# First attention of a four-layer network: weighing one unit later, output rows transposed in the bank of the sums, and preparation work as single steps inside the loop

## The chip, the core and the metric

The kernel runs on one core of a Trainium2 chip. The metric is the device time of one execution in microseconds (us). A core has five engines with a queue of instructions each: TensorE (PE; the profile lists its weight loads apart, as PEld), VectorE (DVE), ScalarE (ACT), GpSimd (POOL) and SyncE (SP), which here only starts transfers. Every queue runs in order; an instruction that needs another engine's result waits on a semaphore, and all that stands behind it in its queue waits with it. Matmuls read SBUF and write PSUM, which is divided into banks of 512 float32 values per partition.

## The reference: what is computed

Four layers follow one another. Each computes a mixing part s and a gate part from the layer-normed input xn, and adds `x + s * silu(ffn(xn))`. The change lies in the first layer and in work that prepares weights for the later ones. The first layer's s is a sliding-window attention over 8 sequences of 512 tokens with 128 features, 16 heads of 8 features and blocks of 64 queries, each of which sees its own block of keys and the block before:

```
q, k, v = proj(Wq, bq), proj(Wk, bk), proj(Wv, bv)      # 16 heads of 8
scores = einsum("bhnqd,bhnkd->bhnqk", qb, kw) * hd ** -0.5   # 64 queries x 128 keys
valid = (t <= s_ + W) & (t >= s_ + 1) & (n * W - W + t >= 0)
attn = softmax(where(valid, scores, -1e9))
out = einsum("bhnqk,bhnkd->bhnqd", attn, vw) ; return out @ Wo.T + bo
```

The first layer's gate part uses six 128x128 weights that come as integers and are decoded: `(q / 7.5 - 1) * scale`. The second layer mixes each token with the one before it (`hidden * time_mix + shifted * (1 - time_mix)`), which the kernel folds into scaled weight copies. The fourth layer's attention uses 16 sigmoid and softplus values per head (mu, sigma, eta, gamma, nu).

## The kernel before

`network` loads x in 8 parts, the constants of all layers, and the attention weights; then it runs `layer_norm`, the preparations `l0_decode`, `l2.fill` and `l1.fill`, `l0_attention`, `l0_ffn`, and from there the later layers. The data lie with features on partitions and tokens along the free axis.

Two kinds of order meet. Instructions that go through `net.in_order(engine)` stay on their queue in the order in which the program makes them. All others (plain `nc.vector`, `nc.scalar`) are placed by a scheduler, among the ordered ones. The layer norm and the attention are ordered. The decoding (`l0_decode`, L2828 to L2830, tile wt from f_q and sc), and the scalars of the fourth layer (`l3_scalars`, from L2875, tiles sp and mu) are free, so the scheduler puts them early: into the layer norm and in front of the attention. The mixing weights of the second layer (`L1Consts.fill`, tiles td, rest and wm, and the halved fourth weight) are ordered on ACT, before the attention, and the two large expert weights (m1_w13 and m1_w2, 2560 and 1280 KB, tile m_w) are started from ACT's queue.

The attention works in 64 units: sequence (batch) b, pair m of query blocks, and half hh of the heads; eight units are one batch. Unit u goes through these steps:

- `scores(u)`: four matmuls into one sc tile of two banks (two such tiles); DVE scales and masks (e<-sc), finds the row maximum (mx), POOL subtracts it. Runs three units ahead.
- Exp on ACT, two units ahead.
- `turned(u)`: eight transposes into two tp tiles, each copied by ACT to pt.
- `weigh(u)`: 32 small matmuls of pt with the values vw, into the tile av: the sums of 16 heads and, in a ninth column, their total. Its two halves alternate between pairs.
- After the second unit of a pair: `norm` (DVE rec and o), `out_rows` (one transpose tpo, and ACT's copy with a bias to ot), and after the last pair of a batch `finish` (ps_o and DVE s).
- `project(b + 1)` makes the next batch's keys, queries and values a step per unit: ps_k with four masked key copies kb (DVE, ACT, DVE, ACT), ps_q with ACT q, and two ps_v with ACT vw.

PSUM's eight banks are used up: four for sc, three in rotation for tp, tpo, ps_k, ps_q, ps_v and ps_o, one for the sums.

The loop gives the order in all queues; an iteration is turned(u), norm, scores(u + 3), out_rows, Exp(u + 2), weigh(u), finish, and one step of project:

```
for u in range(N + 2):
    ended = u >= 1 and u <= N and u % 2 == 0
    if u < N: pts = turned(u)
    if ended: o = norm(u - 1)
    if u + AHEAD < N: scores(u + AHEAD)
    if ended: out_rows(u - 1, o)
    if u + 2 < N: act.activation(e[u + 2], e[u + 2], AF.Exp)
    if u < N: weigh(u, pts)
    if u >= U and u % U == 1: finish(u // U - 1)
    next(todo, None)
```

Of the kernel before, what the change touches and what calls it, by code (L numbers as in the profile page):

```python
# [257 lines left out]
def l0_attention(net, xn, s_out, p0, w, bias):  # L258
# [6 lines left out]
    with ExitStack() as st:  # L265
# [23 lines left out]
        sums = p_av.tile([P, 2, H, HD + 1], F32, tag="av", name="av")  # L289
# [6 lines left out]
        def project(b):  # L296
# [6 lines left out]
            for c in range(4):  # L303
                hm, hb = net.hm4[:, c : c + 1], kbias[:, c : c + 1]
                if c % 2:
                    act.activation(kb[b][:, c, :], ps, AF.Identity, scale=hm, bias=hb)
                    yield
                else:
                    dve.tensor_scalar(kb[b][:, c, :], ps, hm, hb, ALU.mult, ALU.add)
            ps = p_t.tile([P, S], F32, tag="t", name="ps_q")  # L310
# [47 lines left out]
        def turned(u):  # L358

            pts = []  # L360
            for g in range(2):
# [3 lines left out]
                pt = p3.tile([P, 4, P], F32, tag="pt", name="pt")  # L365
# [28 lines left out]
        def out_rows(u, o):  # L394
            b, m = u // U, u // 2 % 4
            tp = p_t.tile([P, 4, P], F32, tag="t", name="tpo")
            pe.transpose(tp[:, 0, :], o.rearrange("p h d -> p (h d)"), net.ident)
            if m == 0:
                ot[b] = p2.tile([P, S], F32, tag="ot", name="ot")

            act.activation(ot[b][:, ts(m, P)], tp[:, 0, :], AF.Identity, bias=bias[:, 2:3])
# [12 lines left out]
        act.activation(e[1], e[1], AF.Exp)  # L414
        todo = iter(())
        for u in range(N + 2):
            if u < N and u % U == 0 and u // U + 1 < B:
                todo = project(u // U + 1)
            ended = u >= 1 and u <= N and u % 2 == 0
            if u < N:  # L420
                pts = turned(u)
            if ended:
                o = norm(u - 1)
            if u + AHEAD < N:
                scores(u + AHEAD)
            if ended:
                out_rows(u - 1, o)
            if u + 2 < N:
                act.activation(e[u + 2], e[u + 2], AF.Exp)
            if u < N:  # L430
                weigh(u, pts)
            if u >= U and u % U == 1:
                finish(u // U - 1)
            next(todo, None)
            if u == 4 * U:
# [3 lines left out]
            if u > 4 * U and u % U == 6:  # L439
                next(low, None)  # L440

# [290 lines left out]
class L1Consts:  # L732
    E = 8

    def __init__(self, net, st):
        nc, tc, E = net.nc, net.tc, self.E
        self.net = net
        self.p1 = p1 = st.enter_context(tc.tile_pool(name="a1_c", bufs=1))
# [7 lines left out]
    def fill(self):  # L746
        net, nc, p1, E = self.net, self.net.nc, self.p1, self.E
        act = net.in_order(nc.scalar)
        self.w13 = net.load(p1, "m1_w13", act)
        self.w2 = net.load(p1, "m1_w2", act)  # L750

        w, par = self.w, self.par
        self.td = td = p1.tile([P, 1], F32, tag="td", name="td")
        act.activation(td, par[:, 0:1], AF.Exp)
        act.activation(td, td, AF.Copy, scale=-1.0)
        self.tf = par[:, 1:2]
        self.wm = wm = p1.tile([P, 3, 2, P], F32, tag="wm", name="wm")
        self.rest = rest = p1.tile([P, 3], F32, tag="rest", name="rest")
        act.activation(rest, par[:, 2:5], AF.Identity, scale=-1.0, bias=net.ones[:, 0:1])
        for i in range(3):  # L760
            act.activation(wm[:, i, 0, :], w[:, i, :], AF.Copy, scale=par[:, 2 + i : 3 + i])
            act.activation(wm[:, i, 1, :], w[:, i, :], AF.Copy, scale=rest[:, i : i + 1])
        act.activation(w[:, 3, :], w[:, 3, :], AF.Copy, scale=0.5)
# [22 lines left out]
        nc.gpsimd.memset(self.keep[:, :, 0:1], 0.0)  # L786

# [554 lines left out]
class L2Consts:  # L1342
# [4 lines left out]
    def __init__(self, net, st):  # L1347
# [5 lines left out]
        self.p1 = p1 = st.enter_context(tc.tile_pool(name="a2_c", bufs=1))  # L1353
# [1442 lines left out]
class Prepared:  # L2796
# [29 lines left out]
    def l0_decode(self):  # L2826
        nc, wt, qw, sc = self.net.nc, self.f0_wt, self.qw, self.sc
        nc.vector.tensor_copy(wt, qw)  # L2828
        nc.vector.tensor_scalar(wt, wt, 1.0 / 7.5, -1.0, ALU.mult, ALU.add)
        nc.vector.tensor_tensor(wt, wt, sc, ALU.mult)  # L2830
# [34 lines left out]
    def l3_scalars(self):  # L2865
# [9 lines left out]
        nc.vector.scalar_tensor_tensor(sp, raw, -1.0, raw, ALU.mult, ALU.min)  # L2875
        nc.scalar.activation(sp, sp, AF.Exp)
        nc.scalar.activation(sp, sp, AF.Ln, bias=net.ones[:, 0:1])
        nc.vector.scalar_tensor_tensor(sp, raw, 0.0, sp, ALU.max, ALU.add)
        sig2, eta2, gam2, nu = (sp[:, i, :] for i in range(4))

# [4 lines left out]
        nc.scalar.activation(mu, par[:, 0, :], AF.Exp, scale=-1.0)  # L2885
        nc.vector.tensor_scalar(mu, mu, 1.0, None, ALU.add)
        nc.vector.reciprocal(mu, mu)
        nc.vector.tensor_scalar(mu, mu, 1e-4, None, ALU.add)
        nc.vector.tensor_scalar(nmu, mu, -1.0, None, ALU.mult)

        nc.vector.tensor_scalar(v_e2, nmu, 2.0, None, ALU.mult)
        nc.vector.reciprocal(v_e2, v_e2)
        nc.vector.tensor_tensor(v_e2, v_e2, sig2, ALU.mult)
        nc.vector.tensor_tensor(v_0, eta2, gam2, ALU.add)
        nc.vector.tensor_tensor(v_0, v_0, v_e2, ALU.subtract)
        nc.vector.tensor_scalar(coef, nu, float(DH), -0.5, ALU.add, ALU.mult)
        nc.vector.tensor_tensor(coef, coef, par[:, 5, :], ALU.mult)


        norm_0 = vec("norm_0")  # L2900
# [124 lines left out]
```

## Time and profile before

| | |
|---|---|
| median of 9 runs | 2329.14 us (2323.07 to 2332.13) |
| profiled execution: time, span | 2332.06 us, 2330.3 us |
| busy in the span | PE 2180.1 (94%), DVE 2003.8, ACT 1846.5, POOL 1571.0 us |
| layer norm ends, first ps_k | 29.91 us |
| first scores of the attention | 42.6 us |
| ps_k of the next batches | 55.95, 97.95, 129.79, 161.7 us, then about 193.6, 226, 259 |
| first feed-forward matmul | 321.26 us |
| PE busy from 42.6 to 319.4 | 259.59 of 276.80 us, mean granted clock 0.92 |

The profile shows each instruction with its start, length, tiles (output <- inputs), shape and, in square brackets, how long its engine stood before it and whom it waited for. A granted clock of 1.00 is the full speed of TensorE, 0.50 half of it. In the windows, the columns are the busy times and counts of PE, PEld, DVE, ACT and POOL, then the granted clock, the share of the transfer engines and GB/s. The chain of waits lists start, length and what the time went to, in the chain that ended last. The page's first lines and its slices for the span:

```profile
span 2330.3 us, 48928 instructions
...
PE 2180.1 (94%) x17762; PEld 1523.3 (65%) x17762; DVE 2003.8 (86%) x3595; ACT 1846.5 (79%) x3882; POOL 1571.0 (67%) x1410
...
PE   5999998999987999869999999999999999999998
...
PEclk7899989899998999989999999999999999999998
```

A slice is 58 us, so the first holds the layer norm and the lead-in, and the next five the attention.

### The profile page before, as it was taken

How to read it: one execution, taken by the hardware profiler on the slowest of the kernel's cores; microseconds unless marked ns; L12 is line 12 of the kernel's file. 1: busy time of each engine (PE TensorE's matmuls, PEld its weight loads, DVE VectorE, ACT ScalarE, POOL GpSimd, SP SyncE). 2: the span in 40 equal slices, each digit the busy share in tenths (PEclk: the TensorE clock that was granted, in tenths of full speed). 3: DMA queues.
4: the chain of work that ended last, by engine and by line, in shares of the span. 5: the costliest groups of instructions: out<-in, count | busy, mean ns of one | idle time of the engine just before them, and what ended most of it. 6: DMA issues, size and time to landing. Idle time of an engine off the chain costs nothing.

```text
span 2330.3 us, 48928 instructions
## 1 busy us (share of the span) xinstructions
PE 2180.1 (94%) x17762; PEld 1523.3 (65%) x17762; DVE 2003.8 (86%) x3595; ACT 1846.5 (79%) x3882; POOL 1571.0 (67%) x1410
## 2 busy tenths in 40 slices
PE   5999998999987999869999999999999999999998
PEld 4666675656634666636777777777777777777796
DVE  4577769785687999659999999999999999999885
ACT  4566655555544899838999999999999999999974
POOL 5344436264276788656788788888788888788644
PEclk7899989899998999989999999999999999999998
DMA  4000000012210000234433444434444444443100
GB/s 144 2 2 2 2 1 23 17 54 70 46 50 16 3 17 16 81 84 108 106 100 92 111 114 105 106 92 107 109 108 105 100 105 107 102 102 101 46 1 37
DMA packets 91618, 156.94 MB, mean 67 GB/s; under 512 B 20145, under 2 KB 44465, under 8 KB 91121
## 3 DMA queue, kind: packets, MB, share of 16 engines
q1 hardware_dynamic: 86736, 140.95, 23.2%
q0 software_dynamic: 4352, 8.92, 1.5%
q10 hardware_dynamic: 288, 3.93, 0.4%
q8 instruction: 142, 2.33, 0.4%
q14 instruction: 100, 0.81, 0.1%
HBM read 30.52 MB, written 12.06 MB: 18 GB/s over the span
## 4 chain that ended last, share of the span: by engine, by line
PE 55%; DVE 28%; POOL 7%; issue 4%; ACT 4%; DMA 2%; SPq 1%; DVEq 0%; ACTq 0%; POOLq 0%
PE sc L84 10%; DVE sc L84 7%; DVE r L84 6%; DVE y L84 6%; PE ps_av L84 5%; PE tp L84 5%; PE ps_kq L84 4%; PE ps_u L84 4%; PE av L84 3%; PE ps_ab L84 3%; PE ps_n L84 2%; DVE mx L84 2%; DVE e L84 2%; PE ps_v L84 2%; POOL yr L84 2%
## 5 line engine op out<-in xcount | busy, mean ns | idle before, releaser
L84 POOL TENSOR_TENSOR ek<-E,kn 128x512 f32<-128x512 f32 (+3 forms) x512 | 433.6, 869 | 204.1 <-DMA kn<-nr 186.0
L84 POOL TENSOR_TENSOR e<-e,mx 128x1024 f32<-128x1024 f32 x112 | 212.1, 1899 | 188.4 <-DVE mx L84 95.5
L84 PE MATMUL sc<-r 128*128 128x512 f32 (+3 forms) x1024 | 312.5, 449 | 25.9 <-DVE y L84 23.0
L84 POOL TENSOR_TENSOR r<-r,rs 128x1024 f32<-128x1024 f32 x128 | 303.7, 2374 | 23.8 <-DMA rs<-r 20.9
L84 PE MATMUL ps_av<-u,at 128*128 128x128 f32 x2560 | 306.8, 275 | 0.3 <-DVE at L84 0.3
L84 PEld LDWEIGHTS ps_av<-u,at 128*128 128x128 f32 x2560 | 296.1, 192 | 1.5 <-ACT at L84 0.8
L84 PEld LDWEIGHTS sc<-r 128*128 128x128 f32 x1024 | 166.7, 193 | 191.4 <-issue 123.6
L84 ACT ACTIVATE y<-y,mn 128x384 f32<-128x384 f32 (+3 forms) x512 | 288.5, 569 | 4.0 <-DVE mn L84 3.2
L84 DVE CUSTOM_DVE_ANT_0 y<-y,ps_g,ncs 128x256 f32<-128x256 f32 (+3 forms) x512 | 253.8, 541 | 0.8 <-ACT y L84 0.8
L84 DVE SCALAR_TENSOR_TENSOR y<-sc,qn,V 128x512 f32<-128x512 f32 (+3 forms) x512 | 246.8, 544 | 8.6
L84 ACT ACT_TABLE_LOAD x179 | 229.7, 1283 | 6.1 <-DVE ex L84 2.1
L84 PEld LDWEIGHTS tp<-ident,y 128*128 128x128 f32 x1280 | 161.0, 141 | 112.3 <-issue 48.5
L84 PE MATMUL tp<-ident,y 128*128 128x128 f32 x1280 | 202.5, 274 | 2.6 <-ACT o L84 2.0
L84 DVE SCALAR_TENSOR_TENSOR sc<-sc,ek 128x1280 f32<-128x1280 f32 x128 | 189.7, 1482 | 9.7 <-PE sc L84 3.1
L84 ACT COPY at<-tp 128x512 f32<-128x512 f32 x376 | 191.3, 509 | 7.6 <-PE tp L84 3.5
L84 DVE TENSOR_TENSOR sc<-sc,EF 128x1280 f32<-128x1280 f32 x128 | 191.9, 1499 | 4.3
L84 ACT ACTIVATE y<-y 128x1280 f32<-128x1280 f32 x128 | 163.4, 1277 | 6.0 <-DVE y L84 2.9
L84 DVE TENSOR_TENSOR r<-sn,ps_kq 128x1024 f32<-128x1024 f32 x128 | 155.1, 1212 | 9.9 <-ACT sq L84 9.9
L84 ACT ACTIVATE sq<-ps_kq 128x1024 f32<-128x1024 f32 x128 | 131.5, 1027 | 35.4 <-PE ps_kq L84 35.4
L84 DVE TENSOR_TENSOR r<-ct,ps_kq 128x1024 f32<-128x1024 f32 x128 | 155.1, 1212 | 0.0
L84 POOL TENSOR_TENSOR s<-s,o 128x512 f32<-128x512 f32 x116 | 148.2, 1277 | 2.5 <-ACT o L84 2.4
L84 ACT ACTIVATE e<-e 128x1024 f32<-128x1024 f32 x112 | 117.3, 1061 | 40.4 <-POOL e L84 40.0
(462 smaller groups left out, 5012.5 us busy)
## 6 DMA issues: line engine op xcount, KB each, us to landing
rs<-r SPq DMA_DIRECT2D x256, 256.0 KB, 3.8
kn<-nr SPq DMA_DIRECT2D x512, 64.0 KB, 2.0
yrows<-yy SPq DMA_DIRECT2D x36, 128.0 KB, 1.8
ct<-trig SPq DMA_DIRECT2D x16, 256.0 KB
EF<-E SPq DMA_DIRECT2D x16, 256.0 KB, 2.5
EF<-E SPq DMA_DIRECT2D x16, 192.0 KB
m_w<-m_w ACTq DMA_DIRECT2D x1, 2560.0 KB, 10.2
x<-x SPq DMA_DIRECT2D x8, 256.0 KB, 4.7
```

Source lines behind the costliest of these rows:

```text
L84: ins = op(*args, **kwargs)
```

## The change

- The loop weighs unit u - 1 in iteration u. The pt tiles come from a ring of four in place of three; the steps that follow the weighing (norm, out_rows, finish) move back by one iteration, and the loop is one longer.
- tpo has no bank of its own. It becomes 128 columns behind the sums, in their tile (`both`, named av).
- The key copies are made in the order ACT, DVE, ACT, DVE, with a pause of project after each DVE copy.
- Decoding, the mixing weights and the scalars become generators whose instructions are ordered on their queues; the loop takes one of their 17 steps in three iterations of every batch from u = 9. The last operation of the decoding goes from DVE to POOL. The low-rank steps come one iteration earlier.
- The constants of the second and third layer are loaded after those of the first, and the two large expert weights are started from SP's queue.

```diff
--- before.py
+++ after.py
@@ -255,7 +255,7 @@
             )
 
 
-def l0_attention(net, xn, s_out, p0, w, bias):
+def l0_attention(net, xn, s_out, p0, w, bias, l1):
 
 
     nc, tc = net.nc, net.tc
@@ -286,7 +286,10 @@
             nc.gpsimd.memset(vw, 1.0)
             vws.append(vw)
 
-        sums = p_av.tile([P, 2, H, HD + 1], F32, tag="av", name="av")
+        both = p_av.tile([P, TB], F32, tag="av", name="av")
+        n_av = 2 * H * (HD + 1)
+        sums = both[:, 0:n_av].rearrange("p (m h d) -> p m h d", m=2, h=H)
+        tpo = both[:, n_av : n_av + P]
 
         pe, dve, act, pool = (
             net.in_order(e) for e in (nc.tensor, nc.vector, nc.scalar, nc.gpsimd)
@@ -300,13 +303,13 @@
             pe.matmul(ps, lhsT=w[:, 1, :], rhs=xb, start=True, stop=True)
 
             kb[b] = p2.tile([P, 4, S], F32, tag="kb", name="kb")
-            for c in range(4):
+            for c in (1, 0, 3, 2):
                 hm, hb = net.hm4[:, c : c + 1], kbias[:, c : c + 1]
                 if c % 2:
                     act.activation(kb[b][:, c, :], ps, AF.Identity, scale=hm, bias=hb)
-                    yield
                 else:
                     dve.tensor_scalar(kb[b][:, c, :], ps, hm, hb, ALU.mult, ALU.add)
+                    yield
             ps = p_t.tile([P, S], F32, tag="t", name="ps_q")
             pe.matmul(ps, lhsT=w[:, 0, :], rhs=xb, start=True, stop=True)
             q[b] = p2.tile([P, S], F32, tag="q", name="q")
@@ -362,7 +365,7 @@
                 tp = p_t.tile([P, 4, P], F32, tag="t", name="tp")
                 for j in range(4):
                     pe.transpose(tp[:, j, :], e[u][:, 4 * g + j, :], net.ident)
-                pt = p3.tile([P, 4, P], F32, tag="pt", name="pt")
+                pt = p5.tile([P, 4, P], F32, tag="pt", name="pt")
                 act.copy(pt, tp)
                 pts.append(pt)
             return pts
@@ -393,12 +396,11 @@
 
         def out_rows(u, o):
             b, m = u // U, u // 2 % 4
-            tp = p_t.tile([P, 4, P], F32, tag="t", name="tpo")
-            pe.transpose(tp[:, 0, :], o.rearrange("p h d -> p (h d)"), net.ident)
+            pe.transpose(tpo, o.rearrange("p h d -> p (h d)"), net.ident)
             if m == 0:
                 ot[b] = p2.tile([P, S], F32, tag="ot", name="ot")
 
-            act.activation(ot[b][:, ts(m, P)], tp[:, 0, :], AF.Identity, bias=bias[:, 2:3])
+            act.activation(ot[b][:, ts(m, P)], tpo, AF.Identity, bias=bias[:, 2:3])
 
         def finish(b):
             ps = p_t.tile([P, S], F32, tag="t", name="ps_o")
@@ -412,32 +414,43 @@
             scores(u)
         act.activation(e[0], e[0], AF.Exp)
         act.activation(e[1], e[1], AF.Exp)
+        def early():
+            yield from net.prep.l0_decode(dve, pool)
+            yield from l1.mixing(act)
+            yield from net.prep.l3_scalars(dve, act)
+
+        rest = early()
         todo = iter(())
-        for u in range(N + 2):
+        pts = {}
+        for u in range(N + 3):
             if u < N and u % U == 0 and u // U + 1 < B:
                 todo = project(u // U + 1)
-            ended = u >= 1 and u <= N and u % 2 == 0
+            ended = u >= 3 and u % 2 == 1
             if u < N:
-                pts = turned(u)
+                pts[u] = turned(u)
             if ended:
-                o = norm(u - 1)
+                o = norm(u - 2)
             if u + AHEAD < N:
                 scores(u + AHEAD)
             if ended:
-                out_rows(u - 1, o)
+                out_rows(u - 2, o)
             if u + 2 < N:
                 act.activation(e[u + 2], e[u + 2], AF.Exp)
-            if u < N:
-                weigh(u, pts)
-            if u >= U and u % U == 1:
+            if 1 <= u <= N:
+                weigh(u - 1, pts.pop(u - 1))
+            if u >= U and u % U == 2:
                 finish(u // U - 1)
             next(todo, None)
+            if u >= U and u % U in (1, 3, 6):
+                next(rest, None)
             if u == 4 * U:
                 low = net.prep.l0_low_rank(
                     p0, lambda name: p_t.tile([P, S], F32, tag="t", name=name), pe, dve, act
                 )
-            if u > 4 * U and u % U == 6:
+            if u > 4 * U and u % U == 5:
                 next(low, None)
+        for _ in rest:
+            pass
 
 
 L0_FFN = (
@@ -735,7 +748,10 @@
     def __init__(self, net, st):
         nc, tc, E = net.nc, net.tc, self.E
         self.net = net
-        self.p1 = p1 = st.enter_context(tc.tile_pool(name="a1_c", bufs=1))
+        self.p1 = st.enter_context(tc.tile_pool(name="a1_c", bufs=1))
+
+    def load(self):
+        net, nc, p1, E = self.net, self.net.nc, self.p1, self.E
         self.rw = net.load(p1, "m1_r")
         self.eb = p1.tile([P, E], F32, tag="eb", name="eb")
         nc.sync.dma_start(self.eb, net.ins["m1_eb"].partition_broadcast(P))
@@ -745,22 +761,8 @@
 
     def fill(self):
         net, nc, p1, E = self.net, self.net.nc, self.p1, self.E
-        act = net.in_order(nc.scalar)
-        self.w13 = net.load(p1, "m1_w13", act)
-        self.w2 = net.load(p1, "m1_w2", act)
-
-        w, par = self.w, self.par
-        self.td = td = p1.tile([P, 1], F32, tag="td", name="td")
-        act.activation(td, par[:, 0:1], AF.Exp)
-        act.activation(td, td, AF.Copy, scale=-1.0)
-        self.tf = par[:, 1:2]
-        self.wm = wm = p1.tile([P, 3, 2, P], F32, tag="wm", name="wm")
-        self.rest = rest = p1.tile([P, 3], F32, tag="rest", name="rest")
-        act.activation(rest, par[:, 2:5], AF.Identity, scale=-1.0, bias=net.ones[:, 0:1])
-        for i in range(3):
-            act.activation(wm[:, i, 0, :], w[:, i, :], AF.Copy, scale=par[:, 2 + i : 3 + i])
-            act.activation(wm[:, i, 1, :], w[:, i, :], AF.Copy, scale=rest[:, i : i + 1])
-        act.activation(w[:, 3, :], w[:, 3, :], AF.Copy, scale=0.5)
+        self.w13 = net.load(p1, "m1_w13")
+        self.w2 = net.load(p1, "m1_w2")
 
         def counting(tag, shape, pattern, base=0, channel=0):
             i = p1.tile(shape, I32, tag=tag + "_i", name=tag + "_i")
@@ -784,6 +786,24 @@
         self.keep = p1.tile([P, E, NTILE], F32, tag="keep", name="keep")
         nc.gpsimd.memset(self.keep, 1.0)
         nc.gpsimd.memset(self.keep[:, :, 0:1], 0.0)
+
+    def mixing(self, act):
+        net, p1, w, par = self.net, self.p1, self.w, self.par
+        self.td = td = p1.tile([P, 1], F32, tag="td", name="td")
+        act.activation(td, par[:, 0:1], AF.Exp)
+        act.activation(td, td, AF.Copy, scale=-1.0)
+        yield
+        self.tf = par[:, 1:2]
+        self.wm = wm = p1.tile([P, 3, 2, P], F32, tag="wm", name="wm")
+        self.rest = rest = p1.tile([P, 3], F32, tag="rest", name="rest")
+        act.activation(rest, par[:, 2:5], AF.Identity, scale=-1.0, bias=net.ones[:, 0:1])
+        yield
+        for i in range(3):
+            act.activation(wm[:, i, 0, :], w[:, i, :], AF.Copy, scale=par[:, 2 + i : 3 + i])
+            act.activation(wm[:, i, 1, :], w[:, i, :], AF.Copy, scale=rest[:, i : i + 1])
+            yield
+        act.activation(w[:, 3, :], w[:, 3, :], AF.Copy, scale=0.5)
+        yield
 
 
 def l1_layer(net, x, xn, s_out, consts, l2):
@@ -1350,7 +1370,10 @@
             self.W, self.H, self.HD, self.LH, self.LD, self.NL, self.CH
         )
         self.net = net
-        self.p1 = p1 = st.enter_context(tc.tile_pool(name="a2_c", bufs=1))
+        self.p1 = st.enter_context(tc.tile_pool(name="a2_c", bufs=1))
+
+    def load(self):
+        net, p1 = self.net, self.p1
         self.w = net.load(p1, "a2_w")
         self.wqt = net.load(p1, "a2_qt")
         self.wg = net.load(p1, "a2_g")
@@ -2823,11 +2846,14 @@
             )
         self.f0_wt = p1.tile([P, 6, P], F32, tag="wt", name="wt")
 
-    def l0_decode(self):
-        nc, wt, qw, sc = self.net.nc, self.f0_wt, self.qw, self.sc
-        nc.vector.tensor_copy(wt, qw)
-        nc.vector.tensor_scalar(wt, wt, 1.0 / 7.5, -1.0, ALU.mult, ALU.add)
-        nc.vector.tensor_tensor(wt, wt, sc, ALU.mult)
+    def l0_decode(self, dve, pool):
+        wt, qw, sc = self.f0_wt, self.qw, self.sc
+        dve.tensor_copy(wt, qw)
+        yield
+        dve.tensor_scalar(wt, wt, 1.0 / 7.5, -1.0, ALU.mult, ALU.add)
+        yield
+        pool.tensor_tensor(wt, wt, sc, ALU.mult)
+        yield
 
     def l0_low_rank(self, p1, bank, pe, dve, act):
 
@@ -2862,7 +2888,7 @@
             dve.tensor_scalar(w0, w0, mean, None, ALU.subtract)
             yield
 
-    def l3_scalars(self):
+    def l3_scalars(self, dve, act):
 
         net, nc, p1 = self.net, self.net.nc, self.p1
         H, DH = 16, 64
@@ l3_scalars @@
-        nc.vector.scalar_tensor_tensor(sp, raw, -1.0, raw, ALU.mult, ALU.min)
-        nc.scalar.activation(sp, sp, AF.Exp)
-        nc.scalar.activation(sp, sp, AF.Ln, bias=net.ones[:, 0:1])
-        nc.vector.scalar_tensor_tensor(sp, raw, 0.0, sp, ALU.max, ALU.add)
...
+        dve.scalar_tensor_tensor(sp, raw, -1.0, raw, ALU.mult, ALU.min)
+        act.activation(sp, sp, AF.Exp)
+        act.activation(mu, par[:, 0, :], AF.Exp, scale=-1.0)
+        yield
+        act.activation(sp, sp, AF.Ln, bias=net.ones[:, 0:1])
+        yield
+        dve.scalar_tensor_tensor(sp, raw, 0.0, sp, ALU.max, ALU.add)
...
+        yield
+        dve.tensor_scalar(mu, mu, 1.0, None, ALU.add)
+        dve.reciprocal(mu, mu)
...
@@ -2930,13 +2964,13 @@
         with tc.tile_pool(name="prep_0", bufs=1) as p0:
             w0, b0 = net.load(p0, "a0_w"), net.load(p0, "a0_b")
             prep.l0_load(p0)
+            l2.load()
+            l1.load()
             net.layer_norm(x, xn)
-            prep.l0_decode()
             l2.fill()
             l1.fill()
-            l0_attention(net, xn, s, p0, w0, b0)
+            l0_attention(net, xn, s, p0, w0, b0, l1)
             l0_ffn(net, x, xn, s, l1)
-        prep.l3_scalars()
         l1_layer(net, x, xn, s, l1, l2)
         st1.close()
         l2_layer(net, x, xn, l2)
```

More of the change, by code (lines that the diff above doesn't have):

```diff
@@ L2874, in l3_scalars @@
         raw = par[:, 1:5, :]
-        nc.vector.scalar_tensor_tensor(sp, raw, -1.0, raw, ALU.mult, ALU.min)
-        nc.scalar.activation(sp, sp, AF.Exp)
-        nc.scalar.activation(sp, sp, AF.Ln, bias=net.ones[:, 0:1])
-        nc.vector.scalar_tensor_tensor(sp, raw, 0.0, sp, ALU.max, ALU.add)
-        sig2, eta2, gam2, nu = (sp[:, i, :] for i in range(4))
         def vec(tag):
@@ L2884, in l3_scalars @@
         mu, nmu, v_e2, v_0, coef = vec("mu"), vec("nmu"), vec("v_e2"), vec("v_0"), vec("coef")
[L2885 to L2897, printed above, removed]
+        yield
[4 more added lines that the diff above has]
+        act.activation(sp, sp, AF.Ln, bias=net.ones[:, 0:1])
@@ new lines, in l3_scalars @@
+        yield
+        dve.scalar_tensor_tensor(sp, raw, 0.0, sp, ALU.max, ALU.add)
+        sig2, eta2, gam2, nu = (sp[:, i, :] for i in range(4))
+        yield
+        dve.tensor_scalar(mu, mu, 1.0, None, ALU.add)
+        dve.reciprocal(mu, mu)
+        dve.tensor_scalar(mu, mu, 1e-4, None, ALU.add)
+        dve.tensor_scalar(nmu, mu, -1.0, None, ALU.mult)
+        dve.tensor_scalar(v_e2, nmu, 2.0, None, ALU.mult)
+        dve.reciprocal(v_e2, v_e2)
+        dve.tensor_tensor(v_e2, v_e2, sig2, ALU.mult)
@@ L2900, in l3_scalars @@
+        yield
+        dve.tensor_tensor(v_0, eta2, gam2, ALU.add)
+        dve.tensor_tensor(v_0, v_0, v_e2, ALU.subtract)
+        dve.tensor_scalar(coef, nu, float(DH), -0.5, ALU.add, ALU.mult)
+        dve.tensor_tensor(coef, coef, par[:, 5, :], ALU.mult)
+        yield
         norm_0 = vec("norm_0")
-        nc.vector.tensor_tensor(norm_0[0:64], nu[0:64], v_e2[0:64], ALU.mult)
-        nc.vector.tensor_tensor(norm_0[64:128], nu[64:128], v_0[64:128], ALU.mult)
+        dve.tensor_tensor(norm_0[0:64], nu[0:64], v_e2[0:64], ALU.mult)
@@ L2903, in l3_scalars @@
+        dve.tensor_tensor(norm_0[64:128], nu[64:128], v_0[64:128], ALU.mult)
         cs, ncs, inv_cs, g_v = vec("cs"), vec("ncs"), vec("inv_cs"), vec("g_v")
-        nc.vector.scalar_tensor_tensor(cs, coef, -1.0, coef, ALU.mult, ALU.max)
-        nc.vector.tensor_scalar(cs, cs, 1e-18, 2e-18, ALU.is_lt, ALU.mult)
-        nc.vector.tensor_tensor(cs, cs, coef, ALU.add)
-        nc.vector.tensor_scalar(ncs, cs, -1.0, None, ALU.mult)
-        nc.vector.reciprocal(inv_cs, cs)
-        nc.vector.tensor_scalar(g_v, coef, -1.0, -0.5 * DH, ALU.mult, ALU.add)
@@ L2912, in l3_scalars @@
-        nc.vector.tensor_tensor(g_v, g_v, inv_cs, ALU.mult)
+        yield
+        dve.scalar_tensor_tensor(cs, coef, -1.0, coef, ALU.mult, ALU.max)
+        dve.tensor_scalar(cs, cs, 1e-18, 2e-18, ALU.is_lt, ALU.mult)
+        dve.tensor_tensor(cs, cs, coef, ALU.add)
+        dve.tensor_scalar(ncs, cs, -1.0, None, ALU.mult)
+        dve.reciprocal(inv_cs, cs)
+        dve.tensor_scalar(g_v, coef, -1.0, -0.5 * DH, ALU.mult, ALU.add)
+        dve.tensor_tensor(g_v, g_v, inv_cs, ALU.mult)
         self.scalars = nu, nmu, v_e2, v_0, norm_0, ncs, inv_cs, g_v
+        yield
```

## The prediction

> **What bounds the kernel now.** I read the slices of the page, then the chain of waits through the first 58 us, the windows of the attention, and its timeline instruction by instruction. The change touches only what lies before 321.3 us, where the first matmul of the first feed-forward part starts; nothing behind that point is edited, except that some small work has been done earlier in both kernels.
>
> The chain of waits, start and length, in the layer norm and the lead-in to the attention:
>
> ```profile
> 13.04 4.84 DMA f_q<-f_q
> 32.75 0.95 DVE wt L2830
> 34.50 1.75 ACT wm L84 x6
> 37.13 1.28 ACT L2877
> 38.79 1.28 ACT L2885
> ```
>
> The timeline of one unit that ends a pair of units, and the next unit's start:
>
> ```profile
> 121.80 0.14 PEld L84 LDWEIGHTS tpo<-ident,o 128*128 128x128 f32 x1 [1.10 <-PE sc L84]
> 121.83 0.30 PE L84 MATMUL tpo<-ident,o 128*128 128x128 f32 x1 [0.24 <-DVE o L84]
> 122.06 1.11 PE L84 MATMUL av<-vw,pt 128*64 128x9 f32 x32
> 122.17 0.37 ACT L84 ACTIVATE ot<-tpo,a_b 128x128 f32<-128x128 f32 x1 [0.87 <-PE tpo L84]
> ```
>
> The attention by windows: us, then busy time of PE, PEld, DVE, ACT and POOL with counts, then the granted TensorE clock:
>
> ```profile
> 62.19:65.61 3.42, 2.08 (x29) 0.86 (x27) 3.28 (x6) 1.83 (x4) 1.90 (x1) 1.00 0.01 2
> 65.61:69.02 3.41, 3.41 (x26) 2.24 (x24) 1.08 (x1) 1.50 (x3) 1.90 (x1) 0.50 0.00 0
> ...
> 106.40:138.20 31.80, 30.47 (x408) 19.93 (x408) 23.50 (x28) 20.74 (x34) 15.17 (x8) 1.00 0.01 2
> ...
> 164.59:168.00 3.41, 2.69 (x42) 1.83 (x38) 3.10 (x4) 1.76 (x3) 0.78 (x2) 1.00 0.00 0
> 304.54:307.95 3.41, 2.73 (x59) 2.41 (x58) 2.17 (x2) 2.38 (x4) 2.23 (x2) 1.00 0.00 0
> 307.95:311.36 3.41, 3.41 (x37) 3.05 (x37) 0.55 (x2) 2.08 (x3) 0.93 (x1) 0.50 0.02 5
> ```
>
> Three things are to be seen. The lead-in is bound by DVE and ACT work that the attention doesn't need at once: a cast that waits for the f_q transfer, six mixing-weight copies, two table loads. The attention itself is bound by PE: of 31.80 us (one batch of 8 units) PE is busy 30.47. And the granted clock is 1.00 or 0.50, nothing between, and changes on a grid of 3.413 us. The two windows of the attention proper that PE had filled for only 2.08 and 2.73 us were followed by half clock, the first for six windows (65.61 to 86.09), the second for five; yet the window with 2.69 kept it. So a gap on PE may cost more than its own length.
>
> **Part 1, the lead-in.** Decoding leaves DVE's queue in the layer norm. PE stood from 15.5 to 19.2 us there, behind a DVE that stood 2.29 us for f_q and then did 0.56 and 0.55 us of wt. I take the norm to end 5.4 us earlier (ps_k at 24.5 in place of 29.91); the bounds are 3.4 (2.29 + 0.56 + 0.55) and 5.4. From ps_k to the first sc there were 12.7 us (29.91 to 42.6). Without wm (1.75), both table loads (2.56), sp, mu, td and rest (0.26 + 0.22 + 0.28), the waits between DVE and ACT that go with them, and the issue of two transfers by ACT (1.86 us from 29.28), there remain ps_k about 1.9, four key copies one behind the other (2 x 0.81, 2 x 0.78, since both engines read one bank in turn in both kernels) and q and v beside them: about 5.9. POOL's masks and ones, 5.5 us behind the norm, end no later than that (29.8 against 30.4). First sc at 30.4: **-12.2 us**; bounds -9 and -13. That ACT begins the key copies is worth nothing here, as the copies stay serial.
>
> The two weight transfers (2560 and 1280 KB) move to SP's queue, behind the small loads. SP carries nothing else that the attention waits for; they are first read at 430 us. Nothing. If they stood ahead of x, whose wait cost 4.2 us, it would show, but x is issued first.
>
> **Part 2, the new waits of the attention.** Weighing a unit later gives the pt copies a whole unit of time, with four buffers for pt in place of three. The row of waits for it looks large (PEld av for ACT pt, 29.6 us in 39 waits), but that is the weight loader, standing while sc still ran. PE itself stood 0.30 us a batch (133.11: idle 0.30 for ACT pt). Gain 0.30.
>
> Against it, tpo now lies in the bank of the sums. In the changed program the weighing that follows tpo waits for ACT's ot copy, as bank mates are one tile. Before, nobody waited for ot: av started at 122.06 while ot ran from 122.17 to 122.54. Now av starts at about 122.58: 0.52 us at each of 4 tpo a batch, **+2.08**. All of PE's later work is queued behind it. Bounds: 0 (if the wait were covered) and 0.87 (ot's longest delay in these rows, 0.37 + 0.50).
>
> With the first key copy on ACT, DVE's kb waits for ACT's, which waits for ps_k. At the second unit of a batch DVE's rec and o stand behind that kb: ps_k + 0.78 + 0.81 + 0.25 + 0.29 = 2.13, against tp + sc = 2.05 on PE, plus the semaphore steps of about 0.1 each; tpo comes about 0.45 late, **+0.45** a batch (bounds 0 and 0.81, a whole kb). The 0.48 us that tp stood for DVE s at 136.21 moves with the finish to the next unit and I find a like wait there for ACT q; no change. A batch so costs 31.85 - 0.30 + 2.08 + 0.45 = 34.08, **+2.2**.
>
> A rule bears on this. The page "PSUM — Partial Sum Buffer" of the Trainium skill (section "PSUM bank collisions raise a hardware error") says that accesses of two engines must be kept apart by bank and quadrant, not by address. The trace agrees so far as the two key copies of one bank never overlap (DVE 130.96 to 131.77, ACT from 131.81). By addresses alone tpo and the sums would not meet, the 2.08 would be nothing and a batch would cost 32.0.
>
> **Part 3, the single steps.** 17 steps, three a batch, done by the seventh batch: DVE's cast and scaling 1.11 us, POOL's multiply (0.95 on DVE, at most 1.9 like POOL's e), ACT's 2.6 us of mixing and exponentials, and some 25 DVE operations of 0.1 to 0.3. DVE (23.50 of 31.80), ACT (20.74) and POOL (15.17) have the room; but each step stands ahead of some pt, e or o. The Ln step carries two table loads, 2.56 us on ACT in one place, ahead of a pt. Ends: 0 and 5.2 (2.6 + 2.56); I take **+3**, two for Ln and one for the rest.
>
> **Part 4, without the clock.** Before, the six batches from 55.95 to 259 took 203.05 us, of which the one from 55.95 to 97.95 took 42.0 against 31.85: 10.1 lost, 1.2 to a wait of tpo for kb and the rest to half clock. The half clock from 307.95 to 321.3 lost 37% of 13.3 = 4.9: at half clock a unit is tp 1.84 + sc 1.91 + av 1.82 and its share of projections and tpo, about 6.4, at full about 4.0. If the clock never fell in the changed kernel: -12.2 - 10.1 - 4.9, +13.2 for six batches, +5.1 for the last two (2 x 2.08 + 0.45, and 0.5 for one more iteration), +3 = **-6**.
>
> **Part 5, the clock.** In the changed kernel's second unit of a batch PE stands 0.24 + 0.45 ahead of tpo and 0.52 behind it, 1.2 us within 2 us, the same as the 1.20 that stood in the window with 2.08 busy. A window over it holds about 2.2. Units that end a pair elsewhere have 0.76 in one place. The nearest row to 2.2 is the one with 2.08, which lost the clock; 2.69 kept it and 2.73 lost it. So I take one loss in each of the six middle batches. A stretch lasts five or six windows, 18.8 us, and costs 37% of that, 7.0: **+42**. Ends: no loss (0) and ten (+70).
>
> The page "TensorE: Matmul & The Clock Gate" (section "Part 1: The HAM clock gate") has the same window, 3.413 us, but lets the clock fall only after a whole window idle. By it none of these gaps would cost the clock and the sum would be -6. The window with 1.34 us idle that lost it says otherwise.
>
> **Sum:** -6 + 42 = +36 against the profiled execution, span 2330.3 and time 2332.06. This run lies 2.9 above the median of 2329.14; carried over, 2329.14 + 36 = 2365 us. A difference below 0.2%, 4.7 us, can't be told from none.
>
> **Rivals.** *A, the clock holds.* PE's gaps stay short of what the gate needs, as at 164.59. Then -6, and -14 if half of the eight batches' ot waits (8 x 1.04) are covered: 2315 to 2323. This is the case on the other side. It decides at one loss: -6 + 7 = +1, two give +8. *B, one loss, or gains and losses that cancel,* for instance a loss at the Ln step alone, where ACT is taken 2.56 us: 2325 to 2334, no change. *C, the waits don't exist:* the bank is shared without the weighing waiting. Then batches cost 32.0 and the time is about 2306; against it stands the wait in the built program, so it has little weight. *D, every batch loses the clock twice,* since a batch has four waits: ten or more losses, 2329 - 6 + 70 = 2393.
>
> **How the numbers follow.** Clock losses in several batches, the forecast: 0.52 (2340 to 2385). D: 0.08. A: 0.28. B: 0.09. C: 0.03. Faster is A and C, 0.31; same is B, 0.09; slower 0.60. The range goes from just under A, 2312 (A with the lead-in's bound of -13 and the steps at nothing would be 2311), to just past D, 2396, since cases of both signs hold most of the chance; a tenth stays outside at each end.
>
> **What would show it.** First sc near 30.4 (part 1). Idle PE ahead of av with ACT ot as releaser, about 0.5 us, four a batch (part 2); if it is missing, C. ps_k every 34 us at clock 1.00 (part 2). Windows of 0.50 in most batches between 60 and 300 us; if the clock is 1.00 throughout, A. Start of the feed-forward part at about 357 in place of 321.3. The rest, from there on, should last the same; if it does not, the prediction is wrong in a place I have not looked at.

## The result and the profile after

The changed kernel takes 2403.21 us (median of 14 runs, 2387.19 to 2424.14) against 2330.36 for the kernel before (43 runs): ratio 1.031, 95% interval 1.0293 to 1.0327, slower by 73 us. Slower was forecast, but at 2365 us in a range of 2312 to 2396. The profiled execution took 2393.02 us, ten less than the median, with a span of 2391.3.

The slices of the page, for the changed kernel:

```profile
span 2391.3 us, 48890 instructions
...
PE   7999999889998799977999999999999999999998
...
PEclk9866767899999899998999999999999999999999
```

The lead-in is shorter than before, and the loss stands where the clock is 6 and 7 tenths, in the slices of the attention. The chain of waits through the lead-in, start and length, no longer holds a DMA, decoding, mixing weights or table loads between the norm and the scores:

```profile
23.72 0.59 ACT xn L84
24.36 1.14 PE ps_k L84 x2
25.57 0.79 ACT kb L84
26.39 0.82 DVE kb L84
...
29.57 1.16 PE sc L84 x16
```

The first scores start at 29.50 in place of 42.6, and the second ps_k at 40.15 in place of 55.95. From there on it goes the other way: ps_k follows at 73.08, 110.75, 152.28, 202.29, 244.94 and 290.97, and the feed-forward part starts at 383.5 in place of 321.3. From that point to the end both spans are alike, 2007.8 against 2009.0 us. So all of the loss lies in the attention.

The second unit of a batch in the timeline of the changed kernel (tpo is named av here, since it lies in that tile):

```profile
75.06 0.81 DVE L84 TENSOR_SCALAR kb<-ps_k,hm,kbias 128x512 f32<-128x512 f32 x1 [0.26 <-ACT kb L84]
75.78 0.25 DVE L84 RECIPROCAL rec<-av 128x16 f32<-128x16 f32 x1
...
76.41 0.33 PE L84 MATMUL av<-ident,o 128*128 128x128 f32 x1 [0.32 <-DVE o L84]
76.78 0.37 ACT L84 ACTIVATE ot<-av,a_b 128x128 f32<-128x128 f32 x1 [0.79 <-PE av L84]
77.29 1.11 PE L84 MATMUL av<-vw,pt 128*64 128x9 f32 x32 [0.55 <-ACT ot L84]
```

The wait that was forecast is there, 0.55 us ahead of the weighing with ACT ot as releaser. It stands ahead of every weighing that follows a tpo, 31 in all: 0.46 us at nearly all of them, 15.0 us together. And the windows, with PE's busy time first and the granted clock behind the five engines:

```profile
75.59:79.01 3.42, 2.55 (x47) 1.87 (x40) 3.28 (x6) 2.38 (x4) 1.31 (x2) 1.00 0.03 5
79.01:82.42 3.41, 3.41 (x30) 1.47 (x28) 3.04 (x3) 2.23 (x3) 1.87 (x1) 0.50 0.00 0
...
181.40:184.81 3.41, 2.95 (x48) 1.76 (x46) 2.52 (x5) 2.56 (x5) 1.90 (x1) 1.00 0.02 5
184.81:188.23 3.42, 3.42 (x16) 1.53 (x15) 0.67 (x1) 1.86 (x4) 1.90 (x1) 0.50 0.01 2
```

The first pair is the unit above, and loses the clock as forecast. The second pair is not a second unit: PE stood only 0.46 us in it, and the clock fell all the same. Between the second ps_k and the feed-forward part, fifteen windows end in such a fall, where there were two before, and 57.6 windows run at half clock, where there were 10.7.

The sum from these rows: the feed-forward part starts 62.2 us later. The second ps_k comes 15.8 earlier. The 46.9 more windows at half clock cost 37% of 3.413 us each, 59 us, by the share that the prediction took. That leaves 62.2 + 15.8 - 59 = 19 us for the waits and the steps themselves.

### The profile page after: what moved, and what is told of

Read it like the earlier page. It is cut to its first block, busy times and chain, and to the rows that moved or that the text cites. A ratio compares the mean times of both kernels' runs of the same rounds, so it can differ in the third digit from the quotient of the medians.

```text
span 2391.3 us, 48890 instructions
## 1 busy us (share of the span) xinstructions
PE 2245.5 (94%) x17762; PEld 1560.8 (65%) x17762; DVE 2012.6 (84%) x3594; ACT 1850.7 (77%) x3882; POOL 1574.1 (66%) x1411
## 4 chain that ended last, share of the span: by engine, by line
PE 61%; DVE 24%; POOL 6%; ACT 4%; issue 3%; DMA 1%; SPq 1%; POOLq 0%; ACTq 0%; DVEq 0%
PE sc L84 12%; DVE sc L84 7%; PE tp L84 6%; PE ps_av L84 6%; DVE r L84 5%; DVE y L84 5%; PE av L84 4%; PE ps_kq L84 4%; PE ps_u L84 4%; PE ps_ab L84 3%; PE ps_n L84 2%; PE ps_v L84 2%; PE ps_o L84 2%; PE ps_y L84 1%; PE ps_k L84 1%
## 5 line engine op out<-in xcount | busy, mean ns | idle before, releaser
L84 DVE SCALAR_TENSOR_TENSOR e<-sc,maskFalse 128x1024 f32<-128x1024 f32 (+1 forms) x96 | 90.4, 952 | 92.4 <-PE sc L84 90.8
L84 PEld LDWEIGHTS av<-vw,pt 128*64 128x64 f32 (+1 forms) x4096 | 104.1, 140 | 73.0 <-issue 45.9
```

The source lines that it names most:

```text
L84: ins = op(*args, **kwargs)
```

## The experiments

Theory 1: the weighing waits for ot since tpo shares the bank of the sums, and the gaps cost the clock. Rival 1: weighing later, with norm behind the key copies, costs the clock. Rival 2: the single steps do. The runs came in three series, the first and the third on chip 2 and the second on chip 5, and in them the kernel before took 2328.6, 2353.6 and 2347.3 us. So each kernel is compared with the kernel before of its own series, by the ratio; differences in us are that ratio or the difference of the two medians, and the two can stand some us apart.

### tpo in a bank of its own

```diff
-            pe.transpose(tpo, o..., net.ident)                # columns behind the sums
+            tp = p_t.tile([P, 4, P], F32, tag="t", name="tpo")
+            tpo = tp[:, 0, :]
+            pe.transpose(tpo, o..., net.ident)
```

> The changed kernel with tpo back in a bank of its own (one of the three rotating ones), all else as changed. Theory 1 (the weighing that waits for ot leaves PE idle 0.5 us four times a batch, and these gaps cost the granted clock): the wait av <- ACT ot is gone, at most four losses of the clock between 40 and 330 us in place of 15, feed-forward part starts near 310, time 2305 to 2330 us. Rival 1 (weighing a unit later and norm behind the key copies cost the clock, the bank has little to do with it): ten or more losses, 2375 to 2410 us. Rival 2 (the single steps on ACT and DVE do it): the same 2375 to 2410, with the gaps of PE at the steps.

Measured: 2334.54 us, ratio 1.0027 (1.0003 to 1.0052), that is 6 us above the kernel before in place of 73. Four losses of the clock behind the lead-in, not 15. PE waits for ot ahead of no weighing any more. Some 67 us hang on the place of tpo, as theory 1 says; both rivals fall as main causes. But the time is 4 us above the expected range, and the 13 us of the lead-in are not seen in it: the last of the four losses lasts 18 windows, from 269.5 us to the end of the attention. Another lies in the steps, as the timeline of this kernel shows:

```profile
235.47 1.90 POOL L84 TENSOR_TENSOR e<-e,mx 128x1024 f32<-128x1024 f32 x1 [2.71 <-DVE v L84]
235.51 1.89 DVE L84 TENSOR_SCALAR coef<-sp 128x16 f32<-128x16 f32 x1
237.43 0.17 DVE L84 TENSOR_TENSOR coef<-coef,par 128x16 f32<-128x16 f32 x1
237.52 0.25 DVE L84 RECIPROCAL rec<-av 128x16 f32<-128x16 f32 x1
...
238.15 0.33 PE L84 MATMUL tpo<-ident,o 128*128 128x128 f32 x1 [2.67 <-DVE o L84]
```

A DVE operation on 16 values per partition takes 1.89 us, ends with POOL's subtraction, and rec and o stand behind it. PE stands 2.67 us, and the batch takes 42.7 us.

### out_rows behind the weighing

```diff
-            if ended:
-                out_rows(u - 2, o)
             if u + 2 < N:
                 act.activation(e[u + 2], e[u + 2], AF.Exp)
             if 1 <= u <= N:
                 weigh(u - 1, pts.pop(u - 1))
+            if ended:
+                out_rows(u - 2, o)
```

> The changed kernel with tpo still in the bank of the sums, but out_rows behind the weighing of its iteration, so that PE goes on with the next unit's transposes while ACT reads tpo. Theory 1: the wait is covered although the bank is shared, PE's gap at tpo falls from 0.5 to at most 0.25 us, two to six losses of the clock, 2310 to 2340 us. Rivals 1 and 2: nothing of theirs is changed, 2375 to 2410 us.

Measured: 2334.50 us, ratio 1.0015 (0.9995 to 1.0034). The bank is shared as in the changed kernel; only what stands behind tpo on PE is different, the next unit's transposes in place of the weighing. That takes away 67 to 69 of 73 us. PE now stands 1.3 us for ot ahead of a weighing in the whole attention, in 2 places, where it was 15.0 us in 31. So it is the wait and not the place in PSUM. In its profiled execution three batches at full clock take 30.6 to 31.2 us, where 31.85 stood before.

### The kernel before with tpo in the bank of the sums

```diff
-        sums = p_av.tile([P, 2, H, HD + 1], F32, tag="av", name="av")
+        both = p_av.tile([P, TB], F32, tag="av", name="av")
+        n_av = 2 * H * (HD + 1)
+        sums = both[:, 0:n_av].rearrange("p (m h d) -> p m h d", m=2, h=H)
+        tpo = both[:, n_av : n_av + P]
...
-            tp = p_t.tile([P, 4, P], F32, tag="t", name="tpo")
-            pe.transpose(tp[:, 0, :], o..., net.ident)
+            pe.transpose(tpo, o..., net.ident)
```

> The kernel before with nothing changed but tpo's place: in the bank of the sums. Theory 1: av waits for ot 0.5 us at each of 32 tpo (17 us in all), and the clock is lost ten times or more (about 40 us): 2370 to 2410 us. Rivals 1 and 2: only the 17 us of waits at most, the clock as before, 2329 to 2347 us.

Measured: 2419.94 us, ratio 1.0372 (1.0339 to 1.0405), 87 to 91 us above the kernel before and 10 above the expected range. This one edit makes the kernel slower than the whole change does. The timeline of one unit and the windows show the same wait and the same fall:

```profile
115.85 0.33 PE L84 MATMUL av<-ident,o 128*128 128x128 f32 x1
116.56 0.39 ACT L84 ACTIVATE ot<-av,a_b 128x128 f32<-128x128 f32 x1
117.00 1.23 PE L84 MATMUL av<-vw,pt 128*64 128x9 f32 x24 [0.83 <-ACT ot L84]
```

```profile
113.89:117.30 3.41, 2.23 (x23) 1.06 (x25) 2.69 (x5) 2.36 (x5) 1.70 (x1) 1.00 0.00 0
117.30:120.72 3.42, 3.42 (x32) 2.26 (x31) 1.22 (x1) 0.61 (x2) 1.89 (x1) 0.50 0.00 0
```

Batches take 45.0 to 48.6 us, with 15 losses behind the lead-in. Theory 1 stands. In all of these kernels tpo and the sums either share a tile and a bank or share neither; what two separate tiles in one bank would do, no run shows.

### The gap filled with work

```diff
             pe.transpose(tpo, o..., net.ident)
+            idle = p_t.tile([P, 4, P], F32, tag="t", name="idle")
+            for j in range(4):
+                pe.transpose(idle[:, j, :], net.ident, net.ident)
```

> The changed kernel with four added transposes of the identity (0.5 us of PE at full clock, into a rotating bank, read by nobody) right behind tpo, so that PE works while it would wait for ot. The work of a batch gets no shorter. Theory 1, in its part on the clock (a gap costs more than its length since the clock falls): at most five losses, the clock near 1.00 from 60 to 320 us, and the time falls to 2320 to 2345 us although PE has 128 instructions more. If the clock falls for another reason than the gap (transposes count little, or the weighings do), it stays at 2385 to 2415 us.

Measured: 2326.09 us, ratio 0.999 (0.9971 to 1.001). The kernel does all that the changed one does and 128 transposes more that nobody reads, and is 75 to 77 us faster. The four transposes take 0.60 us of PE in place of most of the wait:

```profile
77.09 0.60 PE L84 MATMUL idle<-ident 128*128 128x128 f32 x4
```

Three batches in its windows:

```profile
73.59:106.93 33.34, 32.35 (x428) 21.51 (x424) 25.57 (x30) 20.79 (x33) 16.81 (x9) 1.00 0.01 1
106.93:140.27 33.34, 32.36 (x429) 21.49 (x425) 23.52 (x28) 22.30 (x39) 15.45 (x9) 1.00 0.01 2
140.27:173.52 33.25, 32.35 (x428) 21.48 (x425) 23.51 (x28) 22.26 (x39) 15.18 (x8) 1.00 0.01 2
```

A batch is 33.3 us long, 1.5 more than before, so the waits are still paid; but the clock is 1.00. This separates the length of the waits from what they do to the clock. The feed-forward part starts at 315.2 in place of 383.5, with 7.1 windows at half clock in place of 57.6: 68.3 / 50.5 = 1.35 us a window, an estimate that puts the whole difference down to the clock.

### Only some of the gaps filled

```diff
             pe.transpose(tpo, o..., net.ident)
+            if u % U == U - 1:          # second unit's tpo alone; the other kernel: u % U != U - 1
+                idle = p_t.tile([P, 4, P], F32, tag="t", name="idle")
+                for j in range(4):
+                    pe.transpose(idle[:, j, :], net.ident, net.ident)
```

> The changed kernel with the four added transposes only at the tpo of the second unit of a batch (one tpo in four), where the prediction put its one loss a batch. As predicted (only the 1.2 us gap of that unit costs the clock): nearly all losses go, 2322 to 2345 us. Rival (any of the four 0.5 us gaps costs the clock if a window falls badly, which would be why there were 15 losses and not six): eight or more losses remain, 2360 to 2395 us.

> The opposite: the added transposes at the three other tpo of a batch, the gap of the second unit stays. As predicted: one loss in most of the six or seven batches, 2350 to 2375 us. Rival (any gap): fewer losses than the changed kernel by about what the second unit does not cause, 2330 to 2365 us, and this run and the one with the second unit filled together leave more than the 77 us that filling all four took away, or less, if gaps need each other.

Measured: with the second unit's gap filled, 2382.93 us, ratio 1.0153 (1.012 to 1.0187), 36 us above the kernel before; with the three others filled, 2364.99, ratio 1.0076 (1.0051 to 1.0102), 18 us above. So the three gaps that the prediction held harmless cost more together than the one it feared. The first run speaks against "as predicted": six losses remain behind the lead-in, though the rival had eight or more. The second doesn't decide between its two expectations: 2364.99 us lies in both ranges, by the ratio it would be in the rival's alone (2346 against 2328.6), and of its five losses three stand right behind a second unit. The two fills take away 37 and 55 us, together more than the 75 of filling all. So some losses go with either fill; one reading is that a clock that is already lost can't be lost again.

### A fill that uses little of the array

```diff
             pe.transpose(tpo, o..., net.ident)
+            idle = p_t.tile([P, S], F32, tag="t", name="idle")
+            for i in range(2):
+                pe.matmul(
+                    idle[i * W : (i + 1) * W, 0:256], lhsT=net.ident[0:32, 0:W],
+                    rhs=xn[0:32, 0:256], start=True, stop=True,
+                )
```

> The changed kernel with the gap behind tpo filled as before by 0.5 us of work read by nobody, but on a small part of the array: two matmuls of 32 rows and 64 columns of weights with 256 columns, in place of four full 128x128 transposes. So far, of the windows at full clock with 2.80 to 2.97 us of PE busy and 1.35 us or more of weighing, 21 of 23 lost the clock when they held 0.9 us or more of the scores (tiles of 32x64), and 3 of 21 when full-size matmuls stood in their place. Theory 1a (the gate counts how much of the array works, not how long PE is busy): the small fill helps little, eight or more losses, 45 to 80 us above the kernel before. Theory 1b (it counts the time in which PE works): as with the full-size fill, at most five losses, within 10 us of the kernel before.

Measured: 2402.96 us, ratio 1.0231 (1.018 to 1.0282), 49 to 54 us above the kernel before. Nine losses, five of them behind windows in which PE did not stand at all. The fill, and two of these windows with what follows them:

```profile
76.60 0.65 PE L84 MATMUL idle<-xn,ident 32*64 32x256 f32 x4
...
99.04:102.45 3.41, 3.41 (x50) 1.90 (x49) 2.53 (x5) 2.48 (x4) 1.90 (x1) 1.00 0.00 0
102.45:105.87 3.42, 3.42 (x18) 1.48 (x18) 0.55 (x1) 1.95 (x3) 1.89 (x1) 0.50 0.02 5
...
150.24:153.65 3.41, 3.41 (x50) 1.90 (x49) 2.53 (x5) 2.48 (x4) 1.90 (x1) 1.00 0.02 5
153.65:157.07 3.42, 3.42 (x18) 1.48 (x18) 0.54 (x1) 1.95 (x3) 1.90 (x1) 0.50 0.00 0
```

PE is busy 3.41 of 3.41 us, and the clock falls. So it is not idle time alone that the clock follows. The fill on the whole array, 0.60 us where this one has 0.65, held it. Theory 1a is met, though the small fill does take off some 20 of the 73 us.

### The loop as before, with the rest of the change

The loop, tpo's bank and the three pt buffers are those of the kernel before; load order, single steps and ACT's first key copy are those of the change. Two more kernels start from this one.

```diff
-            if u >= U and u % U in (1, 3, 6):                    # lead_no_steps
+            if u >= U and u % U in (1, 3, 6) and steps < 3:
                 next(rest, None)
...
-            for c in (1, 0, 3, 2):                               # lead_old_copies
+            for c in range(4):
```

> The loop of the attention as before (weighing its own unit, tpo in a rotating bank, three pt buffers), with everything else of the change: load order, ACT's first key copy, the single steps. Theory 1: lead-in 11 to 13 us shorter, none of the new losses, one loss at the DVE steps near 235 us (8 us): 2318 to 2332 us. If the steps or the order of the key copies had caused the losses: 2360 to 2400 us.

> lead_only with only the three decoding steps in the loop; the mixing weights and the scalars run behind the loop of the attention. If the steps cost the clock there (batches of 36.3 and 44.5 us where they ran): those batches at about 32 us, feed-forward part 12 to 17 us earlier less 3 to 6 us for the same work behind the loop: 5 to 12 us faster than lead_only, that is 1 to 8 us above the kernel before. If the steps cost no more than their own 3 us: within 4 us of lead_only.

> The kernel with the loop of the attention as before and the rest of the change (lead_only), with the key copies again in the order DVE, ACT, DVE, ACT. If the copy order made the clock fall at the second unit of the first two batches there (33.8 and 34.0 us for a batch where 31.5 stood at full clock): these two batches at 31.5 to 32 us, 4 to 10 us faster than lead_only, which stood 13 us above the kernel before. If it has no part in it: the same as lead_only within 4 us.

Measured: lead_only 2354.01 us, ratio 1.0055 (1.0023 to 1.0087); without the steps 2346.68, 0.9969 (0.9941 to 0.9996); with the old copies 2373.88, 1.0068 (1.0042 to 1.0095). The lead-in is 11.6 us shorter in the first (scores at 31.0), yet the kernel is slower than before, where 2318 to 2332 us had been expected. Without the late steps 0.0086 of the ratio goes, 20 us; by the medians it is 14, since two of the ten runs of lead_only lie 22 us above the others. The expected gain was 5 to 12. So the steps take back what the lead-in gains, or more. Their two batches by windows, first with and then without the steps:

```profile
174.42:210.68 36.26, 34.28 (x418) 22.47 (x414) 24.36 (x29) 25.66 (x40) 15.34 (x9) 0.90 0.01 2
210.68:255.17 44.49, 39.05 (x414) 25.66 (x413) 29.60 (x44) 20.43 (x32) 15.06 (x8) 0.81 0.01 2
```

```profile
175.10:209.00 33.90, 32.68 (x418) 21.65 (x414) 23.57 (x28) 21.68 (x34) 14.87 (x9) 0.95 0.01 2
209.00:243.10 34.10, 32.62 (x416) 21.31 (x412) 25.50 (x32) 21.39 (x33) 15.43 (x9) 0.95 0.01 2
```

The old order of the key copies doesn't help: the expectation that the first two batches would come down to 32 us was wrong (37.2 and 34.1). Whether it costs something stays open, since the intervals of the ratios overlap while the medians stand 13 us apart.

### A version that beats both

```diff
-            if u >= U and u % U in (1, 3, 6):
+            if u >= U and u % U in (1, 3, 6) and (steps < 11 or u >= N - 2):
                 next(rest, None)
+                steps += 1
```

This is added to the kernel with out_rows behind the weighing; the second kernel has the old order of the key copies as well.

> The changed kernel with out_rows behind the weighing, and with the steps from the logarithm on (two table loads, some 20 small DVE operations) taken in the last three iterations and behind the loop, where no exponential follows. In the run with out_rows moved alone, one batch took 39.6 us in place of 31, behind a DVE operation of 128x16 that took 1.9 us while POOL subtracted. Theory 1 with this addition: that loss goes, 8 us, time 2312 to 2326 us, faster than before by 0.2 to 0.8%. If the steps cost nothing there, or cost as much at the end of the loop: 2328 to 2338 us.

> The fastest kernel so far (out_rows behind the weighing, late steps at the loop's end; 0.994 of the kernel before) with the key copies in the old order. If ACT's first copy delays norm and so tpo there as well: 2 to 8 us faster, ratio 0.990 to 0.993. If it is hidden now that tpo stands behind the weighing: the same, 0.993 to 0.995. If ACT's second copy now delays the pt copies of the next unit: slower, 0.995 to 1.000.

Measured: 2335.13 us, ratio 0.994 (0.9918 to 0.9962), and 2327.45 us, ratio 0.9885 (0.9865 to 0.9906). Both are faster than both kernels, by 12 to 14 and 26 to 27 us against the kernel before. The first is as expected by the ratio; the second lies below the 0.990 at which its lowest expectation ended. Whether the second is better than the first for its copies is not settled: they ran on two chips, and in the profiled executions the feed-forward part starts at 299.9 in the first and 301.8 in the second. The second lost the clock for 11 windows from 37 us, while its undisturbed batches are shorter (29.7, 29.7 and 30.8 against 30.6 to 31.3).

## Why the prediction was right or wrong

**Part 1, the lead-in (-12.2): right.** -13.1 at the first scores, just past the bound of -13. The norm ends at 24.36 (24.5 was taken). The second ps_k gains 2.7 more, probably as the weighing of the first unit no longer stands ahead of it.

**Part 2, the new waits (+2.08 and +0.45 a batch): the first right, the second not seen.** The wait for ot is 0.46 us at most places and 0.55 in the row above, where 0.52 was taken. That it comes from the shared tile and bank is shown by the run with an own bank, and that it is the wait that matters by the run with out_rows moved. The +0.45 was to stand ahead of tpo. There PE stood 0.32 us at the second unit (the row above) and 0.15 at the tpo before it, against 0.24 to 0.25 at two places a batch in the kernel before, so no longer in all. The rule on PSUM in the Trainium skill ("PSUM — Partial Sum Buffer", section "PSUM bank collisions raise a hardware error"), which spoke against the change, led to the right term: tpo and the sums do not share an address, and the wait is paid all the same. Rival C is gone.

**Part 3, the steps (+3): too low.** In the loop of before the late ones cost some 14 to 20 us, in part through the clock (14.7 windows at half clock with them, 10.2 without). The 0.1 to 0.3 us for a small DVE operation held for most, but of those that ran beside POOL's subtraction one of coef took 1.89, one of cs 1.77 and one of mu 1.69.

**Part 4, the sum without the clock (-6): borne out.** The filled kernel, which keeps the clock but for 7.1 windows, stands 2.5 us below the kernel before, with an interval of -6.8 to +2.3. The 19 us of waits and steps, worked out above, stand against 13.2 + 5.1 + 3 = 21.3. Rival A, which rested on a clock that holds, would have been near this.

**Part 5, the clock (+42): the step that failed.** That the clock would fall was right, and so was the price: 37% of a half-clock window, 1.26 us, against some 1.35 from the filled kernel. What failed is the count of losses. "So I take one loss in each of the six middle batches" became 15 losses, above the end of ten that the range was built on; a stretch was shorter than taken (57 windows in 15 stretches, 3.8 each, not 5.5). The extra half-clock windows were 6 x 5.5 - 11 = 22 by the prediction and are 47. The reason is the measure: I ranked windows by PE's busy time (2.08 lost, 2.69 kept, 2.73 lost), so a unit with 0.5 us of idle time, at 2.95, seemed safe. What the runs put in its place is the time of full-size matmuls in the window: between 2.8 and 3.0 us of busy time all 22 windows with less than 1.0 us of it lost the clock, and 2 of 59 with more. The last section has the table. The two windows of 2.69 and 2.73 stood in the prediction with opposite outcomes; that was the sign that the measure didn't order them. Their full-size matmuls take 1.56 us (kept) and 1.23 us (lost), and those of the window with 2.08 take 0.54 us (lost). The page "TensorE: Matmul & The Clock Gate" of the Trainium skill (section "Part 1: The HAM clock gate") would have it that the clock falls after an idle window; the windows that lost it here were up to 100% busy by the trace.

**Rival D** (two losses a batch, 2393) is nearest to what happened, at a chance of 0.08: 15 losses in eight batches, none in one and up to four in another, in shorter stretches than it took. Of the 73 us in the medians, 61 are in the profiled spans; the rest is that the profiled execution was one of the faster.

## What to carry to other kernels

A wait that is harmless by its own length has to be priced by what it does to the clock: look at the windows behind it, and whether PE has full-size matmuls to keep the window up. Columns of one PSUM tile waited for each other here though no address was shared; if two results have to share, put work that needs neither between the read of one and the write of the other. Work that is moved off the lead-in into a loop at its limit isn't free because its engine has room: here 14 to 20 us came of operations that sum to some 10 by the lengths that the prediction gave them.

## What the runs showed of the hardware

**The clock follows full-size matmul work far more than PE's busy time.** For each 3.413 us window from 38 to 335 us that ran at full clock and held scores or weighing, in the fourteen profiles (825 windows, 85 lost the clock behind them), I added the time of matmuls on 128x128 of the array: the transposes, ps_k, ps_q, ps_v, ps_o, the few others of this size, and the full-size fill. The scores (tiles of 32x64) and the weighing (128x64, 9 columns) were left out.

| full-size matmul time in the window | windows | clock lost behind it |
|---|---|---|
| under 1.0 us | 75 | 69 |
| 1.0 to 1.4 us | 267 | 16 |
| 1.4 us and more | 483 | 0 |

By busy time the same windows don't separate: between 2.8 and 3.0 us, 24 of 81 lost it. Busy time isn't without a part: the 16 that lost it with 1.0 us or more were busy at most 3.12 us, and four of the six that kept it with less are windows of the small fill with PE busy throughout. The kernel before lives on the edge: in its steady batches the lowest windows hold 1.04 to 1.09 us (one unit's transposes) and keep the clock. In the changed kernel, with its waits of 0.5 us, seven such windows hold 0.97, and all seven lost it. That a sharp line lies near 1.0 is a reading of these rows; what the runs show directly is the pair of fills, of like length: full-size ones hold the clock, small ones don't. The full-size fill also loads full-size weights (0.47 us), so matmuls and weight loads are not told apart.

**A DVE operation can wait inside itself for POOL.** Beside the 1.89 us of the 128x16 TENSOR_SCALAR, the cast of 128x768 took 1.77 us in the changed kernel with POOL's subtraction beside it, and 0.56 in the layer norm of the kernel before. The end is common (1.89 us ending at 237.40, POOL's at 237.37). In all nine profiles in which this operation starts beside the subtraction it took 1.88 or 1.89 us and ended 0.03 us behind POOL; in the five in which it doesn't, it took 0.11 to 0.17 us. No run changes POOL's work alone. The reductions mx and the key copies kb from PSUM beside the same subtraction kept their 1.22 and 0.81 us.
